# A gated delta-rule block on one Trainium2 core: the weights' preparation moved from a setup stage into the hand-written scheduler

## The chip, the cores and the metric

The kernel runs on one core of one Trainium2 chip. The metric is device microseconds of one execution; three timed executions of the kernel before gave 3868.83, 3886.9 and 3894.53 us, and their median, 3886.9 us, is the time before. A separate execution was recorded by the hardware profiler; the trace and every duration below come from it.

## The reference

Two residual sub-blocks, each with a LayerNorm in front and behind, over x of 8 batches, 1024 tokens, 128 features, all in float32. The first is a gated delta-rule attention with 16 heads (key size 64, value size 128); the second is a small feed-forward mix.

```python
q = l2(silu(causal_conv4(x @ Wq.T, conv_q)));  k = l2(silu(causal_conv4(x @ Wk.T, conv_k)))
v = silu(causal_conv4(x @ Wv.T, conv_v))
alpha = exp(-exp(A_log) * softplus(x @ Wa.T + dt_bias));  beta = 2 * sigmoid(x @ Wb.T)
# per token and head:
S = a_t * (S - b_t * k_t (k_t . S)) + k_t v_t;   o_t = S . q_t
attn = rms_norm(o) @ Wo.T
x = x + layernorm(attn(layernorm(x)))
# feed-forward on y = layernorm(x), y_prev = y shifted by one token:
out = sigmoid((mu_r*y + (1-mu_r)*y_prev) @ W_r.T) * (relu((mu_k*y + (1-mu_k)*y_prev) @ W_k.T)**2 @ W_v.T)
x = x + layernorm(out)
```

## The kernel before

**Tiling.** The recurrence is computed in chunks of 128 tokens. A unit is one batch, one half of its tokens (512) and one group of four heads: 8 x 2 x 4 = 64 units, in that order.

**Setup.** Constants come first: identities, triangular masks, `neg_a`, `dtb`, `mu` (lines 366 to 415). Then, in lines 425 to 480, a pool called `setup` loads all the weights and transposes them on TensorE, since the matmuls need them with the 128 features on the partitions. The three feed-forward matrices go to `wf` and the two gate matrices to `wab`. Wq, Wk (512 KB each), Wv and Wo (1 MB each) come in pieces of 512 KB through a staging tile `wt` (or `wot`) with two buffers, so the third piece's load waits until the first has been transposed. Each PSUM bank of up to four transposes is copied out by ScalarE and VectorE in turn (lines 358 and 360). For each group of four value heads the last is treated otherwise: its four convolution taps are multiplied into the weights by GpSimd (line 462, 16 products in all), transposed, and kept as four matrices in `wv`, so that its convolution is done by TensorE as four accumulated matmuls. The three loads of the taps (line 443) are issued on ScalarE's DMA queue, everything else on SyncE's.

**After the setup** the pool `mem` is opened on the space that `setup` gave up. GpSimd zeroes `tt` (two buffers), `tn` and `xs16` (line 500), and two DMAs write zeros from `xs16` to a DRAM scratch `td` (line 503).

**The scheduler.** All other work is 16 Python generators ("streams"), interleaved by a planner, class `Flow`, when the kernel is built. Each `yield part(engine, reads, resources, when)` says what the next piece needs: an engine, data written, free buffers of a kind, and a condition. `Flow` keeps a modelled clock per engine. In each turn it works out the earliest start of every stream's next piece, and among those within 0.3 us (`NEAR`) of the earliest it takes the stream that is least advanced by its own "due" count: each stream starts with a given due number and gains 1/parts with each piece. It adds 1.0 us (`SLACK`) between a write and a read on another engine, and it models the TensorE clock in windows of 3.4133 us. The order that results is fixed on every engine's queue; instructions of the streams are emitted through helpers, so the profile gives them all line 234. `begins` (due 1.2) runs once for a batch: it loads x by halves of 512 tokens into `xs` (one buffer), takes mean and variance on VectorE, a power on GpSimd, normalizes, transposes on TensorE into `xnT`, then computes the gates (`wabT` matmuls, softplus, cumulative sums, exponentials, two transposes) and sends `rowd` to DRAM. Only when a batch's `begins` is through may its convolutions (`keys` and `values`, both through `conv`) be placed: `conv` multiplies `xnT` by one transposed weight tile `wT[:, m]` and applies the taps on VectorE. `directs` uses `wv`, and `projects` uses `woT` and, at a half's end, `wfT`.

Staging tiles that the change uses are the scheduler's own: `mt` (two buffers, 128 x 16 x 128, used by `products` to `levels`) and `o` (two buffers, 128 x 4 x 128, used by `norms` and `projects`).

Of the kernel before, what the change touches and what calls it, by code (L numbers as in the profile page):

```python
# [8 lines left out]
F32 = mybir.dt.float32  # L9
AF = mybir.ActivationFunctionType  # L10
ALU = mybir.AluOpType
# [4 lines left out]
P = 128  # L16
H, DK, DV, KW = 16, 64, 128, 4
G = 4
NG = H // G
# [4 lines left out]
NVT = 1  # L24
# [3 lines left out]
NQ = H * DK  # L28
# [6 lines left out]
class Flow:  # L35
# [110 lines left out]
    def give(self, kind, tile_):  # L146
        if tile_.space == PSUM:
            kind, tile_ = self.of.pop(tile_.tensor.name, (kind, tile_))
        self.free.setdefault(kind, []).append(tile_)
# [70 lines left out]
def part(eng, *reads, when=None, spare=0, **takes):  # L220
    return eng, reads, takes, when, spare
# [76 lines left out]
def kernel(  # L298
# [51 lines left out]
    def quads(t):  # L350
        return t.rearrange("p (a b) -> p a b", b=P)

    turn = [0]

    def evac(dst, src):
        turn[0] += 1
        if turn[0] % 2:
            nc.scalar.copy(dst, src)
        else:
            nc.vector.tensor_copy(dst, src)  # L360

    spare = [0]

    def bank(name):
        spare[0] += 1
        return psums[spare[0] % len(psums)][:, 0:512]


    ident = const.tile([P, G, P], F32, tag="ident", name="ident")
    for i in range(G):  # L370
# [51 lines left out]
    woT = const.tile([P, H, D], F32, tag="woT", name="woT")  # L422
    wabT = const.tile([P, 2 * H], F32, tag="wabT", name="wabT")
    wfT = const.tile([P, 3, D], F32, tag="wfT", name="wfT")
    with tc.tile_pool(name="setup", bufs=2) as sp:
        wf = sp.tile([P, 3, D], F32, tag="wf", name="wf", bufs=1)
        for i, w in enumerate((W_r, W_k, W_v)):
            nc.sync.dma_start(wf[:, i, :], w)
        wab = sp.tile([2 * H, D], F32, tag="wab", name="wab", bufs=1)
        nc.sync.dma_start(wab[0:H, :], Wa)  # L430
        nc.sync.dma_start(wab[H : 2 * H, :], Wb)
        pw = bank("pw_ab")
        nc.tensor.transpose(pw[:, : 2 * H], wab, ident1[: 2 * H, : 2 * H])
        nc.vector.tensor_copy(wabT, pw[:, : 2 * H])
        pw = bank("pw_f")
        for i in range(3):
            nc.tensor.transpose(quads(pw)[:, i, :], wf[:, i, :], ident1)
        nc.vector.tensor_copy(wfT, quads(pw)[:, 0:3, :])

        n = 0  # L440
        for name, w, cw in (("q", Wq, conv_q), ("k", Wk, conv_k), ("v", Wv, conv_v)):
            nt = w.shape[0] // P
            nc.scalar.dma_start(taps[:, n : n + nt, :], cw.rearrange("(n p) k -> p n k", p=P))
            for g in range(nt // 8):
                wt = sp.tile([P, 8, D], F32, tag="wt", name=f"wt_{name}{g}")
                nc.sync.dma_start(
                    wt, w[g * 1024 : (g + 1) * 1024, :].rearrange("(n p) d -> p n d", p=P)
                )
                for i in range(2):
                    pw = bank(f"pw_{name}{g}_{i}")  # L450
                    for j in range(4):
                        if name != "v" or j < G - NVT:
                            nc.tensor.transpose(quads(pw)[:, j, :], wt[:, 4 * i + j, :], ident1)
                    if name != "v":
                        evac(wT[:, n : n + 4, :], quads(pw))
                    elif NVT < G:
                        m = 2 * NQ // P + (2 * g + i) * (G - NVT)
                        evac(wT[:, m : m + G - NVT, :], quads(pw)[:, : G - NVT])
                    for j in range(G - NVT if name == "v" else G, G):
                        scaled = sp.tile([P, KW, D], F32, tag="scaled", name=f"ws_{g}{i}{j}")  # L460
                        for k in range(KW):
                            nc.gpsimd.tensor_tensor(
                                scaled[:, k, :], wt[:, 4 * i + j, :],
                                taps[:, n + j, k : k + 1].broadcast_to([P, D]), ALU.mult,
                            )
                        pw = bank(f"pw_t{g}_{i}_{j}")
                        for k in range(KW):
                            nc.tensor.transpose(quads(pw)[:, k, :], scaled[:, k, :], ident1)
                        evac(wv[:, 2 * g + i, :, j - (G - NVT), :], quads(pw))
                    n += 4  # L470
        for g in range(2):
            wot = sp.tile([P, 8, DV], F32, tag="wt", name=f"wot_{g}")
            nc.sync.dma_start(
                wot, Wo[:, g * 8 * DV : (g + 1) * 8 * DV].rearrange("d (h v) -> d h v", v=DV)
            )
            for i in range(2):
                pw = bank(f"pw_o{g}_{i}")
                for j in range(4):
                    nc.tensor.transpose(quads(pw)[:, j, :], wot[:, 4 * i + j, :], ident1)
                evac(woT[:, g * 8 + 4 * i : g * 8 + 4 * i + 4, :], quads(pw))  # L480

    mem = ctx.enter_context(tc.tile_pool(name="mem", bufs=1))
# [64 lines left out]
    stock("rs", 2, [P, NC])  # L549
    stock("st", 2, [P, 6])  # L550

    units = [(b, hf, g) for b in range(B) for hf in range(NH) for g in range(NG)]
    gs = {}
    st = [dict(at=[]) for _ in units]
# [21 lines left out]
    def begins():  # L576
        for b in range(B):
# [25 lines left out]
                give("bank", pt)  # L603
                give("xs", xs)

            yield part("PE", xnT, bank=1)
            pab = take("bank")
            ab = pab[:, : NC * 2 * H].rearrange("p (c k h) -> p c k h", k=2, h=H)
            for c in range(NC):
# [63 lines left out]
    def conv(n, u, done, m=None):  # L673

        b, hf, _ = u
        m = n if m is None else m
        yield part("PE", bank=1, spare=2, when=lambda: len(done) < 2)
        pp = take("bank")
        xT = gs[b]["xnT"][:, KW - 1 + hf * TU : KW - 1 + (hf + 1) * TU]
        pe.matmul(pp, wT[:, m, :], xT, start=True, stop=True)  # L680
        yield part("ACT", pp, acc=1, pb=1)
        acc, pb = take("acc"), take("pb")
        ac.copy(pb[:, KW - 1 :], pp)
        ac.activation(acc, pp, AF.Copy, scale=taps[:, n, KW - 1 : KW])
        give("bank", pp)

        yield part("POOL", *([pb] if hf < NH - 1 else []))
        if hf:
            po.tensor_copy(pb[:, : KW - 1], edge[:, m, :])
        else:  # L690
            po.memset(pb[:, : KW - 1], 0.0)
        if hf < NH - 1:
            po.tensor_copy(edge[:, m, :], pb[:, TU:])
        for j in range(KW - 1):
            yield part("DVE", acc, pb)
            ve.scalar_tensor_tensor(
                acc, pb[:, j : j + TU], taps[:, n, j : j + 1], acc, ALU.mult, ALU.add
            )
        give("pb", pb)
        done.append(acc)  # L700
# [4 lines left out]
    def keys():  # L705
        for n, u in enumerate(units):
            b, hf, g = u
            yield part("PE", when=lambda: b in gs)
            for pr in range(NP):
                yield from conv(NQ // P + g * NP + pr, u, kq_done)  # L710
                yield from conv(g * NP + pr, u, kq_done)
# [97 lines left out]
    def directs():  # L809
        for n, u in enumerate(units):  # L810
            b, hf, g = u
            a = st[n]
            for c in range(CU if NVT else 0):
                t0 = hf * TU + c * P
                yield part("PE", bank=1, when=lambda: "vr" in a)
                xnT = gs[b]["xnT"]
                pv = take("bank")
                for j in range(KW):
                    pe.matmul(
                        pv[:, : NVT * DV], xnT[:, t0 + j : t0 + j + P],  # L820
                        wv[:, g, j].rearrange("p h v -> p (h v)"), start=j == 0, stop=j == KW - 1,
                    )
                yield part("ACT", pv)
                v = a["vr"][:, c, G - NVT :, :]
                ac.activation(v, pv[:, : NVT * DV].rearrange("p (h v) -> p h v", v=DV), AF.Silu)
                give("bank", pv)
                yield part("POOL", v)
                po.tensor_tensor(
                    v, v, a["r"][:, c, G - NVT :, None].broadcast_to([P, NVT, DV]), ALU.mult
                )  # L830
            prog["directs"] += 1
# [404 lines left out]
    def projects():  # L1236
        for u in units:
            b, hf, g = u
            for c in range(CU):
                yield part("PE", when=lambda: normed_outs)  # L1240
                o = normed_outs.pop(0)
                yield part("PE", o, bank=1)
                pt = take("bank")
# [118 lines left out]

    with tc.manual_schedule():
        flow.run([
            (begins(), 4.75, 1.2), (keys(), 25, 0.9), (lengths(), 16, 1.0), (products(), 16, 2.0),
            (rows(), 16, 2.9), (directs(), 12, 2.9), (values(), 19, 2.9), (blocks(), 17, 3.0),
            (decays(), 8, 3.2), (gathers(), 3, 3.2), (scatters(), 3, 3.2), (levels(), 18, 3.5),
            (prepares(), 16, 3.9), (steps(), 26.5, 4.0), (norms(), 32, 4.2), (projects(), 28.75, 4.2),
        ])
# [29 lines left out]
```

## Time and profile before

| what | value |
|---|---|
| timed executions (median) | 3868.83, 3886.9, 3894.53 us (3886.9) |
| profiled execution, own time | 3905.89 us |
| its span in the trace | 3903.8 us |
| DVE, ACT, POOL busy | 69%, 60%, 62% of the span |
| granted TensorE clock, mean | 0.945 of full |
| DMA traffic | 186.28 MB, mean 48 GB/s |

The profiled execution took 2.1 us more than its span, and 19.0 us more than the median. Engines: PE is the matmul part of TensorE and PEld its weight load, DVE is VectorE, ACT ScalarE, POOL GpSimd, SP SyncE. An engine name with a q (SPq, ACTq) is its queue issuing a DMA. A row of the timeline gives start, duration, engine, line, operation, output and inputs, count, and in brackets how long the engine had been idle before and what released it. The table by stretches gives, for each stretch of time, its length, the busy time and instruction count of each engine, the granted clock, the mean busy share of the 16 DMA engines and GB/s.

### The profile page before, as it was taken

Reading aid. Unit: us, or ns where it says so; the run is one execution under the profiler, and the core shown is the slowest. Engines: PE = TensorE matmul, PEld = TensorE weight load, DVE = VectorE, ACT = ScalarE, POOL = GpSimd, SP = SyncE. Lnnn points to the kernel's source line nnn. Section 1 sums busy time; section 2 is a strip of 40 time slices with the busy share of each in tenths; the row PEclk is TensorE's granted clock in tenths of the full one; section 3 lists DMA queues with packets and bytes.
Section 4 is the critical chain, followed back from the end, with each engine's and each line's share of the span. In section 5 each row is a group of like instructions: output and inputs, shape, how many; then the busy total and the mean of one; then the engine's idle time right before and its main releaser. Section 6 shows DMA issues by size and latency. Waiting matters only on the chain. (4 is left out here: it accounts for less than half of the span.)

```text
span 3903.8 us, 126873 instructions
## 1 busy us (share of the span) xinstructions
PE 3497.1 (90%) x52848; PEld 2672.6 (68%) x52848; DVE 2712.1 (69%) x5021; ACT 2323.4 (60%) x5774; POOL 2432.3 (62%) x4369
## 2 busy tenths in 40 slices
PE   5799998999989999999998899888998999989886
PEld 3576776767767776776776677666776667766675
DVE  5667667687776777777776677766677677667752
ACT  4466665656657566666656666565565666556452
POOL 3656666576666666667666576656666566666652
PEclk8899998999999999999999999899999999989997
DMA  3222222222222222222222222221222222222210
GB/s 77 54 43 42 56 47 47 52 45 49 51 50 46 54 46 44 58 52 42 50 54 44 45 51 48 48 48 38 56 44 51 48 42 51 51 41 49 46 36 11
DMA packets 712863, 186.28 MB, mean 48 GB/s; under 512 B 573120, under 2 KB 679008, under 8 KB 712288
## 3 DMA queue, kind: packets, MB, share of 16 engines
q1 hardware_dynamic: 708144, 178.11, 22.1%
q8 instruction: 415, 6.80, 0.7%
q14 instruction: 160, 1.31, 0.1%
q10 hardware_dynamic: 4144, 0.07, 0.1%
HBM read 138.18 MB, written 23.07 MB: 41 GB/s over the span
## 5 line engine op out<-in xcount | busy, mean ns | idle before, releaser
L234 DVE SCALAR_TENSOR_TENSOR acc<-pb,taps,acc 128x512 f32<-128x512 f32 x1344 | 1102.9, 823 | 211.5 <-ACT acc L234 105.1
L234 PE MATMUL bank<-xnT,wT 128*128 128x512 f32 x886 | 496.9, 649 | 12.2 <-ACT acc L234 5.3
L234 POOL TENSOR_TENSOR qk<-qk,egb 128x256 f32<-128x256 f32 x256 | 213.9, 836 | 450.4 <-PE pair L234 428.0
L234 POOL TENSOR_TENSOR vr<-vr,r 128x128 f32<-128x128 f32 (+1 forms) x448 | 355.4, 797 | 208.7 <-ACT vr L234 207.1
L234 POOL TENSOR_TENSOR nb<-nb,tmp 128x14 f32<-128x14 f32 (+6 forms) x896 | 334.7, 374 | 70.2
L234 ACT COPY pb<-bank 128x512 f32<-128x512 f32 x443 | 257.6, 581 | 202.6 <-PE bank L234 156.2
L234 POOL TENSOR_TENSOR tmp<-nb 128x14 f32<-128x14 f32 (+6 forms) x896 | 327.4, 365 | 48.1
L234 ACT COPY o<-pair 128x512 f32<-128x512 f32 x256 | 150.1, 586 | 340.4 <-PE pair L234 250.5
L234 DVE TENSOR_TENSOR_SCAN at<-at,ident 128x512 f32<-128x512 f32 x256 | 337.0, 1317 | 20.8 <-DMA at<-rowd 20.0
L234 PEld LDWEIGHTS bank<-tn,mt 64*64 64x64 f32 (+1 forms) x14192 | 282.9, 112 | 91.9 <-issue 25.0
L234 ACT ACTIVATE junk<-o 128x128 f32<-128x128 f32 x1024 | 317.3, 310 | 28.3
L234 PE MATMUL pair<-vr,tt 128*128 128x128 f32 x2048 | 297.6, 291 | 40.0 <-ACT tt L234 35.1
L234 PE MATMUL bank<-tn,mt 64*64 64x64 f32 (+1 forms) x14192 | 315.9, 191 | 19.4 <-DVE tn L234 4.7
L234 POOL TENSOR_TENSOR o<-o,so 128x512 f32<-128x512 f32 x256 | 320.8, 1253 | 19.1
L234 PE MATMUL bank<-woT,oT 128*128 128x128 f32 x2040 | 293.6, 288 | 20.8 <-ACT oT L234 16.9
L234 PEld LDWEIGHTS pair<-vr,tt 128*128 128x128 f32 x2048 | 264.5, 202 | 68.7 <-ACT tt L234 38.4
L234 PEld LDWEIGHTS bank<-woT,oT 128*128 128x128 f32 x2040 | 259.5, 197 | 72.8 <-ACT oT L234 24.6
L234 ACT ACTIVATE acc<-bank,taps 128x512 f32<-128x512 f32 x443 | 307.1, 693 | 0.3
L234 PE MATMUL pair<-w,at 128*128 128x128 f32 x2048 | 296.6, 290 | 2.3 <-issue 1.9
L234 PE MATMUL pair<-qk 64*128 64x256 f32 x2048 | 293.3, 405 | 4.8 <-ACT o L234 2.6
L234 POOL TENSOR_TENSOR so<-so,mhalf 128x4 f32<-128x4 f32 x256 | 280.4, 1095 | 20.1
L234 PEld LDWEIGHTS pair<-w,at 128*128 128x128 f32 x2048 | 262.5, 199 | 31.8 <-issue 20.8
(235 smaller groups left out, 7524.7 us busy)
## 6 DMA issues: line engine op xcount, KB each, us to landing
at<-rowd SPq DMA_DIRECT2D x256, 256.0 KB, 3.3
egb<-rowd SPq DMA_DIRECT2D x512, 64.0 KB, 3.2
tq<-td SPq DMA_DIRECT2D x256, 64.0 KB, 2.6
tt<-tq SPq DMA_DIRECT2D x256, 64.0 KB, 2.4
md<-mt SPq DMA_DIRECT2D x512, 16.0 KB, 1.8
nb<-md SPq DMA_DIRECT2D x64, 128.0 KB, 2.1
td<-nb SPq DMA_DIRECT2D x128, 64.0 KB, 3.1
xs<-in_L_attn_x_dram SPq DMA_DIRECT2D x16, 256.0 KB
```

The source lines that it names most:

```text
L234: res = call(*args, **kw)
```

## The change

The setup pool goes, with its helpers `evac` and `bank`. A 17th stream, `weights`, does the same loads, transposes and copies through the planner, with due number 0.0 and 1000 parts, so its count stays below that of every other stream. The taps' loads move from ScalarE's queue to SyncE's. Wk and Wq are loaded into one `mt` tile and all of Wv into the other, with no wait between them; Wo goes into the second when Wv has been transposed. The small matrices share one `o` tile, and the scaled value weights use the other. Key and query weights are transposed two at a time, in turn. A set `loaded` gates the streams that need weights, piece by piece.

```diff
-    with tc.tile_pool(name="setup", bufs=2) as sp:
-        wf = sp.tile([P, 3, D], F32, tag="wf", name="wf", bufs=1)
...
-                evac(woT[:, g * 8 + 4 * i : g * 8 + 4 * i + 4, :], quads(pw))
+    loaded = set()
+
+    def weights():
+        n = 0
+        yield part("SP")
+        for cw in (conv_q, conv_k, conv_v):
+            nt = cw.shape[0] // P
+            sy.dma_start(taps[:, n : n + nt, :], cw.rearrange("(n p) k -> p n k", p=P))
+            n += nt
+        yield part("SP", o=1)
+        small = take("o")
+        sy.dma_start(small[0:H, 3], Wa)
+        sy.dma_start(small[H : 2 * H, 3], Wb)
+        for i, w in enumerate((W_r, W_k, W_v)):
+            sy.dma_start(small[:, i], w)
+        yield part("PE", small[: 2 * H, 3], bank=1)
+        pw = take("bank")
+        pe.transpose(pw[:, : 2 * H], small[: 2 * H, 3], ident1[: 2 * H, : 2 * H])
+        yield part("DVE", pw)
+        ve.tensor_copy(wabT, pw[:, : 2 * H])
+        give("bank", pw)
+        loaded.add("ab")
+
+        yield part("SP", mt=2)
+        first, second_ = take("mt"), take("mt")
+        wide = lambda w: w.rearrange("(n p) d -> p n d", p=P)
+        nq = NQ // P
+        sy.dma_start(first[:, :nq], wide(Wk))
+        sy.dma_start(first[:, nq:], wide(Wq))
+        for i in range(2):
+            half_ = slice(i * nq, (i + 1) * nq)
+            sy.dma_start(second_[:, half_], wide(Wv[i * NQ : (i + 1) * NQ, :]))
+        last = G - NVT
+        for i in range(4):
+            for k in range(2):
+                m = (1 - k) * nq + 2 * i
+                yield part("PE", first[:, k * nq + 2 * i], bank=1)
+                pw = take("bank")
+                for j in range(2):
+                    pe.transpose(quads(pw)[:, j, :], first[:, k * nq + 2 * i + j], ident1)
+                yield part(("ACT", "DVE")[k], pw)
+                copy = (ac.copy, ve.tensor_copy)[k]
+                copy(wT[:, m : m + 2, :], quads(pw)[:, 0:2])
+                give("bank", pw)
+                loaded.update((m, m + 1))
+        give("mt", first)
+        for g in range(NG):
+            yield part("PE", second_[:, g * G], bank=1)
...
+            loaded.update(range(m, m + last))
+            for j in range(last, G):
+                yield part("POOL", second_[:, g * G + j], o=1)
+                scaled = take("o")
+                for k in range(KW):
+                    po.tensor_tensor(
+                        scaled[:, k, :], second_[:, g * G + j],
+                        taps[:, 2 * nq + g * G + j, k : k + 1].broadcast_to([P, D]), ALU.mult,
+                    )
...
+            loaded.add(("v", g))
+        yield part("SP")
+        for g in range(NG):
+            sy.dma_start(
+                second_[:, g * G : (g + 1) * G],
+                Wo[:, g * G * DV : (g + 1) * G * DV].rearrange("d (h v) -> d h v", v=DV),
+            )
...
+            loaded.add(("o", g))
+        give("mt", second_)
...
-            yield part("PE", xnT, bank=1)
+            yield part("PE", xnT, bank=1, when=lambda: "ab" in loaded)
...
-        yield part("PE", bank=1, spare=2, when=lambda: len(done) < 2)
+        yield part("PE", bank=1, spare=2, when=lambda: len(done) < 2 and m in loaded)
...
-                yield part("PE", bank=1, when=lambda: "vr" in a)
+                yield part("PE", bank=1, when=lambda: "vr" in a and ("v", g) in loaded)
...
-                yield part("PE", when=lambda: normed_outs)
+                yield part("PE", when=lambda: normed_outs and ("o", g) in loaded)
...
-            (begins(), 4.75, 1.2), (keys(), 25, 0.9), (lengths(), 16, 1.0), (products(), 16, 2.0),
+            (weights(), 1000, 0.0), (begins(), 4.75, 1.2), (keys(), 25, 0.9), (lengths(), 16, 1.0), (products(), 16, 2.0),
```

More of the change, by code (lines that the diff above doesn't have):

```diff
@@ L351, in quads @@
         return t.rearrange("p (a b) -> p a b", b=P)
[L353 to L366, printed above, removed]
     ident = const.tile([P, G, P], F32, tag="ident", name="ident")
@@ L424 @@
     wfT = const.tile([P, 3, D], F32, tag="wfT", name="wfT")
-    with tc.tile_pool(name="setup", bufs=2) as sp:
-        wf = sp.tile([P, 3, D], F32, tag="wf", name="wf", bufs=1)
[L427 to L479, printed above, removed]
-                evac(woT[:, g * 8 + 4 * i : g * 8 + 4 * i + 4, :], quads(pw))
@@ L550 @@
     stock("st", 2, [P, 6])
+    loaded = set()
[44 more added lines that the diff above has]
+            yield part("PE", second_[:, g * G], bank=1)
+            pw = take("bank")
+            for j in range(last):
+                pe.transpose(quads(pw)[:, j, :], second_[:, g * G + j], ident1)
+            yield part("ACT", pw)
+            m = 2 * nq + g * last
+            ac.copy(wT[:, m : m + last, :], quads(pw)[:, :last])
+            give("bank", pw)
+            loaded.update(range(m, m + last))
[7 more added lines that the diff above has]
+                    )
+                yield part("PE", scaled, bank=1)
+                pw = take("bank")
+                for k in range(KW):
+                    pe.transpose(quads(pw)[:, k, :], scaled[:, k, :], ident1)
+                give("o", scaled)
+                yield part("DVE", pw)
+                ve.tensor_copy(wv[:, g, :, j - last, :], quads(pw))
+                give("bank", pw)
+            loaded.add(("v", g))
[5 more added lines that the diff above has]
+            )
+        yield part("PE", small, bank=1)
+        pw = take("bank")
+        for i in range(3):
+            pe.transpose(quads(pw)[:, i, :], small[:, i], ident1)
+        give("o", small)
+        yield part("DVE", pw)
+        ve.tensor_copy(wfT, quads(pw)[:, 0:3, :])
+        give("bank", pw)
+        for g in range(NG):
+            yield part("PE", second_[:, g * G], bank=1)
+            pw = take("bank")
+            for j in range(G):
+                pe.transpose(quads(pw)[:, j, :], second_[:, g * G + j], ident1)
+            yield part("ACT", pw)
+            ac.copy(woT[:, g * G : (g + 1) * G, :], quads(pw))
+            give("bank", pw)
+            loaded.add(("o", g))
+        give("mt", second_)
```

## The prediction

> **What bounds the kernel now.** I read the page first, then the table by stretches for the batches, then the first 53 us in the timeline. The page's line of engines:
>
> ```profile
> PE 3497.1 (90%) x52848; PEld 2672.6 (68%) x52848; DVE 2712.1 (69%) x5021; ACT 2323.4 (60%) x5774; POOL 2432.3 (62%) x4369
> ```
>
> TensorE is the bound over the whole. The stretches below are cut where each batch's last output goes out (650.04, 1107.01, 1575.83, 2046.39, 2521.99, 2989.30, 3474.07 and 3900.36 us in the timeline of SyncE's queue):
>
> ```profile
> 650.00:1107.00 457.00, 422.75 (x6365) 324.55 (x6364) 332.33 (x615) 292.94 (x733) 304.58 (x543) 0.98 0.24 49
> 1107.00:1576.00 469.00, 426.61 (x6785) 325.54 (x6785) 341.94 (x629) 284.90 (x706) 301.70 (x537) 0.96 0.24 49
> 2046.00:2522.00 476.00, 435.32 (x6601) 332.78 (x6603) 337.45 (x627) 289.37 (x721) 305.54 (x544) 0.95 0.23 48
> 2989.00:3474.00 485.00, 440.63 (x6638) 338.57 (x6626) 345.97 (x636) 291.55 (x726) 306.33 (x546) 0.95 0.23 48
> ```
>
> In the steady state PE is busy for 91 to 93% of each batch. But batches of equal work take 457 to 485 us: the planner's order differs from batch to batch. All this comes after the part that the change touches, which is the start:
>
> ```profile
> 0.00:27.00 27.00, 12.95 (x64) 10.01 (x64) 5.96 (x12) 5.55 (x10) 8.82 (x37) 0.94 0.52 128
> 27.00:53.00 26.00, 8.18 (x36) 6.58 (x35) 7.60 (x30) 5.89 (x13) 7.56 (x10) 0.52 0.13 41
> ```
>
> Two stretches stand one after the other: 27 us of weights with DMA half busy, then 26 us of the first batch's norms and gates, in which no engine is busy for a third of the time and the DMA hardly at all. The timeline says why they do not overlap:
>
> ```profile
> 12.82 2.03 SPq L446 DMA_DIRECT2D wt_v<-in_L_attn_Wv_dram  x2
> 16.78 5.77 POOL L462 TENSOR_TENSOR ws<-wt_v,taps 128x128 f32<-128x128 f32 x16 [13.04 <-DMA wt_v<-in_L_attn_Wv_dram]
> 27.05 0.38 SPq L234 DMA_DIRECT2D xs<-in_L_attn_x_dram  x1
> 27.14 3.56 POOL L500 MEMSET tt<- 128x2048 f32 x2 [4.58 <-PE pair L479]
> 32.07 0.81 SPq L503 DMA_DIRECT2D td<-xs  x2
> 34.83 0.38 SPq L234 DMA_DIRECT2D xs<-in_L_attn_x_dram  x1
> 53.00 8.12 PE L234 MATMUL bank<-xnT,wT 128*128 128x512 f32 x12
> ```
>
> The first x load and the memsets wait for the setup's last transposes, which end at 27.0 us, and whose space they take over. The chain of `begins` is x0 issued at 27.05, x1 at 34.83 (7.8 us later, `xs` having one buffer), first convolution at 53.00 (18.2 us later).
>
> **The change part by part.**
>
> *Removed: the wait for the setup's space.* x0 is then held only by what is ahead of it on SyncE's queue. The constants' four issues end at 2.61. The taps' three issues come over from ScalarE's queue: 0.45 + 0.60 + 1.52 = 2.6 us, to 5.2. Five small matrices took from 2.65 to 5.99, 3.3 us, to 8.5. The planner's 0.5 us an issue puts x0 here, ahead of Wk. So x0 goes out at about 8.5, unless the two zero writes `td` stand in front. They wait for memsets: those take 3.56 + 0.96 + 0.53 = 5.05 us on POOL and can start when its constants end, at 3.7, so they end at 8.8; with 0.8 us for the two writes and 5.9 us of taps and small loads behind, x0 would go out at 15.5. In the trace x0 (27.05) passed `td` (32.07) while its memset was unfinished, so I take 8.5 and keep 15.5.
>
> *Moved: 2 MB of loads beside `begins`.* In the setup, Wq was issued at 6.24 and landed 4.5 us later, and Wk was there by 12.5, so a second 512 KB adds some 1.8 us. Behind x0 (half that size, 0.9 us), Wk and Wq go out at 8.9 and 9.4 and land near 14.3 and 16.1; Wv follows by 20. x0 itself is ahead of them.
>
> *Added waits in the fixed orders.* The planner, with 1.0 us of slack per hop, puts the 16 transposes of Wk and Wq ahead of x0's four transposes on PE. On the chip they wait for Wq: from 16.1, at 0.25 to 0.27 us each (8 in 1.97, 4 in 1.07), they end near 20.3. x0's would have started 6.7 us after the issue (33.71 - 27.05), at 15.2. Queued behind are x0's normalizing (two `xn` buffers) and with it x1's load. This costs `begins` 5 us. On POOL the 16 products (5.77 us) are planned after the first power, and between them it is idle: at worst one group (4 x 0.36 = 1.4 us) stands before the second power. The Wv and Wo transposes, 44 x 0.27 = 12 us, go into 18 us in which PE is mostly idle; copies of 0.5 to 0.7 us on ACT and DVE likewise. For these I take 2.5 us, between 0 and 5.
>
> *Sum.* First convolution: 8.5 + 7.8 + 5 + 18.2 + 2.5 = 42.0 us instead of 53.0: **11 us less**. With no interference: 8.5 + 26 = 34.5, 18.5 us less. With `td` in front and all interference, 15.5 + 7.8 + 5 + 18.2 + 5 = 51.5, 1.5 us less; if in addition the first power were behind the products that need Wv, some 4 us more, a loss of 2.5. From the first convolution on all work follows it, so what is gained there is kept if the order stays as good. Against the profiled execution: 3905.9 - 11 = 3894.9, a factor of 0.9972; on the median, **3876 us**.
>
> *The taps' queue.* ScalarE's queue shows 4144 packets for 0.07 MB, the last third landing 4.3 us after its issue; on SyncE's queue they are ahead of the gate weights and x0. The Trainium skill, page "DMA: Bandwidth & Descriptors", section "Issuing engines are not separate DMA queues", says that issuing from several engines saves only sequencer time, as all transfers run on the same 16 engines. By that the move costs the 2.6 us counted above. That row's 4.3 us allows more: taps issued until 5.2 are done at 9.5, a us after x0's issue, which I leave inside the 2.5 us.
>
> *The TensorE clock.* The granted clock fell from 0.94 in the setup to 0.52 in `begins`, and the first convolutions ran at 0.86 us instead of 0.43. I count nothing for this, as PE has room beside `begins`. The Trainium skill, page "TensorE: Matmul & The Clock Gate", section "HAM oscillation — how this bites in real kernels", says that idle gaps of over about 3.4 us halve the clock; that speaks against scattering transposes, and by it the 44 late ones would take some 0.42 us each (0.42 is the mean of the Wq transposes in the groups by line), 6.6 us more, and the sum would be a gain of 4 us.
>
> *The order of the other 16 streams.* None of their pieces changes, but the planner now reaches the first convolution with other engine clocks and another phase of its windows, and every later choice can fall otherwise. The rows bound this: the six full batches take 457, 469, 470, 476, 467 and 485 us, mean 470.7, standard deviation 9.3. If seven batches were new draws, their sum would move by 9.3 x 2.65 = 25 us, and the difference of two such sums by 35. Matmul counts of 6245 to 6857 in these stretches show that part of the spread is only where the cut falls, so 35 is too much; I take 25. Its mean is nothing.
>
> **The rivals.**
>
> *A better order besides.* A batch of 457 and PE's idle time of 33 to 45 us in a batch show that there is room. 4 us less in each of seven batches, with the 11, makes 39 us, the 1%: some 3840 us. Against it: nothing in the change aims there.
>
> *A worse order.* The place is the steady state, the mechanism the same reshuffled queue order. Batches at 478 instead of 470.7 cost 7 x 7.3 = 51 us, less 11: 3927 us. It decides from 7.1 us a batch on; the slowest row, 485, is twice as far out. Against it: the chance of so many bad batches at once, and PE's 91% leaves only so much to lose.
>
> *No overlap in fact.* If the fixed orders make `begins` wait for the weights piece after piece, the first convolution stays near 51 to 55 us: 3885 to 3890 us.
>
> **How the numbers follow.** Likeliest: 11 us gained, order about as good, 3876 us, 0.53 (3850 to 3905 by itself). Better order 0.24, worse order 0.15, no overlap 0.08. A 1% of 3887 is 39 us, about what a measurement of this kernel can tell from no change. So faster by over 1%: 0.24; within: 0.53 + 0.08 = 0.61; slower: 0.15. The range takes the likeliest case and the nearer half of both orders' cases: 3822 to 3926 us.
>
> **What would show it.** Right: x0's load at 8 to 9 us, x1's at 19 to 24, the first convolution at 38 to 46; transposes of Wk and Wq on PE ahead of x0's, released by a DMA; batches again between 457 and 485. Wrong in the start: `td` before the taps on SyncE's queue, x0 after 15, POOL's power behind the products, or the first convolution after 50. Wrong in the rest: the distance from the first convolution to the end (3850.8 us before) changes by more than 28 us; then the order, not the start, makes the result.

## The result and the profile after

The changed kernel takes 3851.9 us (median of 6 runs, 3844.9 to 3861.1) against 3890.2 us before (6 runs, 3868.8 to 3897.3): a ratio of 0.9907 [0.9887, 0.9928], 0.9% or some 36 to 38 us faster. The forecast was 11 us. The range held the time, and the 1% that the prediction put between "faster" and "no change" was just not reached; the interval crosses it.

The profiled execution took 3852.50 us, its span is 3850.8. Its line of engines on the page:

```profile
PE 3465.8 (90%) x52848; PEld 2662.8 (69%) x52848; DVE 2709.6 (70%) x5021; ACT 2325.4 (60%) x5779; POOL 2433.2 (63%) x4369
```

The same 52848 matmuls kept PE busy 31 us less, and it was idle for 385.0 us instead of 406.7 (span minus busy). The start, from the timeline:

```profile
7.54 0.43 SPq L234 DMA_DIRECT2D xs<-in_L_attn_x_dram  x1
8.11 0.53 POOL L428 MEMSET xs<- 128x512 f32 x1
12.54 2.24 SPq L431 DMA_DIRECT2D td<-xs  x2
12.57 0.69 PE L234 MATMUL bank<-ident,mt 128*128 128x128 f32 x2 [4.58 <-DMA mt<-in_L_attn_Wk_dram]
14.50 2.82 PE L234 MATMUL bank<-ident,mt 128*128 128x128 f32 x12 [1.24 <-DMA mt<-in_L_attn_Wq_dram]
17.12 0.40 PE L234 MATMUL bank<-ident,xn 128*128 128x128 f32 x1
18.89 0.38 SPq L234 DMA_DIRECT2D xs<-in_L_attn_x_dram  x1
34.67 2.03 ACT L234 COPY woT<-bank 128x512 f32<-128x512 f32 x4
36.70 1.28 ACT L234 ACT_TABLE_LOAD   x1
38.00 0.28 ACT L234 ACTIVATE eg<-bank 128x128 f32<-128x128 f32 x1
39.55 7.87 PE L234 MATMUL bank<-xnT,wT 128*128 128x512 f32 x12
```

x0 now goes out at 7.54 us, x1 at 18.89, and the first convolution starts at 39.55 instead of 53.00: 13.45 us earlier. The transposes of Wk and Wq stand ahead of x0's on PE, held by their loads, as forecast. But the rest of the run also became shorter. From the first convolution to the end it took 3850.8 us before and 3811.25 now, 39.6 us less in these two executions. The one of before was 16 us above its median; by the medians, 38 us less in all and 13 at the start, some 25 us are left for the rest. The table by stretches says where they lie; the two stretches are the start, and the last batch from the seventh's last output to its own. Before:

```profile
0.00:53.00 53.00, 21.13 (x99) 16.59 (x99) 13.56 (x42) 11.44 (x22) 16.39 (x47) 0.73 0.33 85
3474.07:3900.36 426.29, 358.77 (x5509) 282.86 (x5507) 235.83 (x457) 220.86 (x579) 226.11 (x398) 0.90 0.18 36
```

and after:

```profile
0.00:39.55 39.55, 19.27 (x99) 16.18 (x99) 12.99 (x42) 12.43 (x26) 16.42 (x47) 0.85 0.45 114
3441.68:3847.51 405.83, 347.19 (x5382) 273.60 (x5381) 234.57 (x455) 221.45 (x580) 227.14 (x398) 0.94 0.19 38
```

The last batch is 20.5 us shorter. PE's idle time there fell from 67.5 to 58.6 us and its busy time by 11.6, with a granted clock of 0.94 instead of 0.90. With 127 fewer matmuls left after the seventh batch's output, some 8 us of the 20.5 (an estimate, 127 at the row's mean of 0.065 us) are work that now lies ahead of the cut. The last batch comes 3400 us after the weights; the planner's order is what reaches so far. That was the theory to test.

### The profile page after: what moved, and what is told of

Its sections match the earlier page's. It is cut to its first block, busy times and chain, and to the rows that moved or that the text cites. A ratio compares the mean times of both kernels' runs of the same rounds, so it can differ in the third digit from the quotient of the medians.

```text
span 3850.8 us, 126886 instructions
## 1 busy us (share of the span) xinstructions
PE 3465.8 (90%) x52848; PEld 2662.8 (69%) x52848; DVE 2709.6 (70%) x5021; ACT 2325.4 (60%) x5779; POOL 2433.2 (63%) x4369
## 5 line engine op out<-in xcount | busy, mean ns | idle before, releaser
L234 DVE SCALAR_TENSOR_TENSOR acc<-pb,taps,acc 128x512 f32<-128x512 f32 x1344 | 1088.7, 812 | 208.5 <-ACT acc L234 108.6
L234 PE MATMUL bank<-xnT,wT 128*128 128x512 f32 x878 | 488.4, 645 | 4.1 <-ACT tt L234 2.7
L234 PEld LDWEIGHTS bank<-tn,mt 32*32 32x32 f32 (+1 forms) x14176 | 281.3, 111 | 96.8 <-issue 26.4
L234 PE MATMUL bank<-tn,mt 32*32 32x16 f32 (+1 forms) x14176 | 314.1, 191 | 20.1 <-ACT acc L234 5.6
L234 PE MATMUL bank<-woT,oT 128*128 128x128 f32 x2032 | 286.6, 285 | 20.5 <-ACT oT L234 17.6
L234 DVE TENSOR_TENSOR mt<-pair,at 128x512 f32<-128x512 f32 x256 | 175.9, 687 | 164.3 <-PE pair L234 105.8
```

The lines of the kernel that those rows point to most:

```text
L234: res = call(*args, **kw)
```

## The experiments

**Crossing start and order.** The streams' order was written down, as the sequence of choices that the planner made in each kernel, and then replayed in place of its own choice. In both kernels the first 38 pieces of `begins` (and, in the changed one, all 52 of `weights`) come before any other stream, so the sequences can be cut there and crossed. Beyond the cut every engine's queue holds the same instructions in the same order as the kernel that it was taken from. The edit in both kernels:

```diff
     def run(self, streams):
...
-            near = min(could)[0] + self.NEAR
-            k = min(x[1:] for x in could if x[0] <= near)[1]
-            s = waiting[k][0]
...
+        for c in ORDER:
+            s, (eng, reads, takes, when, spare) = waiting[c]
...
             need = next(s, None)
```

> The changed kernel with its start (weights beside the first norms and gates), but from the first convolution on every engine's queue in the order of the kernel before. Theory ORDER (13.5 us come from the earlier first convolution, the other 25 from the order in which the other streams now fall): first convolution near 39.6 us, 3890 - 13.5 = 3877 us, ratio 0.9965. Rival START (the overlap itself is worth all 38 us, for example by a warmer clock or a better filled pipeline): 3852 us, ratio 0.991.

Measured: 3875.7 us, ratio 0.9964 [0.9946, 0.9983]; the first convolution at 40.02 us.

> The kernel before with its setup in front, but from the first convolution on every queue in the order of the changed kernel. ORDER: first convolution at 53 us, 3890 - 25 = 3865 us, ratio 0.9936, the last batch shorter than before as in the changed kernel (406 us against 426 between the last two batches' final outputs). START: 3890 us, ratio 1.000.

Measured: 3869.0 us, ratio 0.9944 [0.9923, 0.9965]; the first convolution at 52.94 us. START falls with both. The product of the two ratios is 0.9908, the changed kernel's is 0.9907: start and order add up. The start's part is 0.36% (14 us, by its interval 7 to 21), the order's 0.56% (22 us, 14 to 30); that the order's is the larger is likely, but the intervals overlap. The same two stretches show it, first for the new start with the old order, then for the old start with the new order:

```profile
0.00:40.02 40.02, 19.21 (x98) 16.12 (x99) 12.94 (x42) 12.42 (x26) 16.43 (x47) 0.85 0.45 113
3456.31:3879.51 423.20, 360.06 (x5511) 283.99 (x5509) 235.46 (x457) 220.65 (x579) 224.46 (x397) 0.90 0.18 37
```

```profile
0.00:52.94 52.94, 20.79 (x99) 16.17 (x100) 13.48 (x42) 11.43 (x22) 16.34 (x47) 0.73 0.33 85
3469.28:3872.44 403.16, 347.39 (x5385) 273.27 (x5383) 234.94 (x455) 221.45 (x580) 225.86 (x398) 0.93 0.19 38
```

The first stretch goes with the start (40 or 53 us), the last batch with the order (423 to 426 us or 403 to 406). Between the first convolution and the seventh batch's end the four kernels take 3421, 3416, 3402 and 3416 us (before, new start with old order, after, old start with new order). That stretch does not sort them by order: the two with the same new order differ by 14. Over the whole, PE was busy for 3497.1, 3496.5, 3465.8 and 3477.1 us in the same sequence: 31 of the 32 us that the new order takes off behind the new start, and 20 of the 28 behind the old one, are time in which the same 52848 matmuls ran shorter, not time in which PE waited less. The mean granted clock of the four executions (0.945, 0.946, 0.951, 0.945) goes with this behind the new start alone, so why they ran shorter is not settled.

**Is the better order a merit of the change?** Six kernels, before or after, in which only the planner's modelled clocks begin at another time (0.3, 3.0 and 6.0; 2.1, 2.4 and 8.0), so that its phase and near ties fall otherwise and no work changes:

```diff
-        self.now = dict(PE=0.0, DVE=0.0, ACT=0.0, POOL=0.0, SP=0.0)
+        self.now = dict(PE=0.3, DVE=0.3, ACT=0.3, POOL=0.3, SP=0.3)
```

> The changed kernel, only the planner's modelled clocks begin at 0.3 instead of 0, which redraws the order and leaves the start's work. The planner's own model makes this order 35 us longer than that of the changed kernel (a model's number, not a time). ORDER: the overlap's 13 us remain, the rest is a new draw: 3870 to 3890 us, 3885 if the chip follows the model. START: 3852 us again, within 5.

Measured: 3850.6 us, ratio 0.9898 [0.9876, 0.9920]. It equals the changed kernel, as START said, and ORDER's 3870 to 3890 us was missed, though the crossed kernels speak against START; the planner's model, which made this order longer, was no guide.

> The kernel before, only the planner's modelled clocks begin at 2.4 instead of 0. The planner's model makes this order 19 us shorter (a model's number, not a time). ORDER: some 3871 us, ratio 0.995, with nothing changed in the start. START: 3890 us, ratio 1.000 within 0.002.

Measured: 3875.9 us, ratio 0.9965 [0.9946, 0.9985]: a better order without the change. With two orders of the changed kernel at 3851 us, it stayed open whether the weights' stream as such leads to better orders; four more draws put that question.

> The changed kernel with the planner's modelled clocks beginning at 3.0; the start's work is the same. Theory DRAW (the order gained or lost by a change of phase is a matter of chance, with a spread of some 10 us): anywhere from 3850 to 3885 us, the 13 us of the start kept, so below 3890. Rival SYSTEMATIC (with the weights as a stream the planner always finds an order better by some 25 us): 3851 us within 5, as with the clocks at 0 and 0.3.

Measured: 3882.6 us, ratio 0.9987 [0.9970, 1.0005], although its first convolution starts at 39.69 us.

> As the one with 3.0, the clocks beginning at 6.0. DRAW: 3850 to 3885 us. SYSTEMATIC: 3851 us within 5.

Measured: 3864.5 us, ratio 0.9952 [0.9937, 0.9967].

> The kernel before with the planner's modelled clocks beginning at 2.1. DRAW: 3864 to 3900 us, another value than 3889 and 3876. SYSTEMATIC: 3876 to 3890 us, the orders without the weights' stream staying behind by 25 us once the start's 13.5 us are taken off.

Measured: 3885.1 us, ratio 1.0007 [0.9985, 1.0029].

> The kernel before with the planner's modelled clocks beginning at 8.0. DRAW: 3864 to 3900 us; one of the two draws under 3870 would show that the order of the changed kernel is in reach without the change. SYSTEMATIC: 3876 to 3890 us.

Measured: 3910.9 us, ratio 1.0059 [1.0038, 1.0079], although the planner's model made this order 24 us shorter. That is above DRAW's 3900 us as well, and no draw of the kernel before came under 3870.

SYSTEMATIC falls with the start at 3.0: the same change with another phase gains next to nothing. But these kernels are fewer draws than they look. Before at 2.1, after at 3.0 and after at 6.0 have one and the same order: behind the start, their traces show the same operations on the same tiles in the same sequence on DVE, ACT, POOL and SyncE's queue, and the last batch has the same counts, which differ in every other order. The rows of the last batch for these three, named in that sequence:

```profile
3472.70:3876.14 403.44, 354.23 (x5435) 279.21 (x5435) 241.51 (x465) 222.70 (x584) 238.53 (x401) 0.94 0.19 39
3465.98:3876.07 410.09, 359.81 (x5435) 282.87 (x5435) 241.00 (x465) 222.79 (x584) 238.05 (x401) 0.93 0.19 38
3459.54:3864.84 405.30, 355.26 (x5435) 278.75 (x5435) 240.88 (x465) 222.76 (x584) 237.76 (x401) 0.93 0.19 39
```

So with and without the stream of weights the planner can find this order, here called C, and behind the old start it is no better than the first (1.0007). In one table, with a letter for each order (the crossed kernels have A behind the new start and B behind the old one), with the time from the first convolution to the end of batch 7 and the last batch from each profiled execution:

| kernel, planner's clocks begin at | order | ratio to before | first convolution, us | to the end of batch 7, us | last batch, us |
|---|---|---|---|---|---|
| before, 0 | A | 1 | 53.00 | 3421 | 426 |
| before, 2.1 | C | 1.0007 | 52.86 | 3420 | 403 |
| before, 2.4 | D | 0.9965 | 52.68 | 3413 | 404 |
| before, 8.0 | E | 1.0059 | 52.62 | 3432 | 427 |
| after, 0 | B | 0.9907 | 39.55 | 3402 | 406 |
| after, 0.3 | F | 0.9898 | 39.86 | 3401 | 401 |
| after, 3.0 | C | 0.9987 | 39.69 | 3426 | 410 |
| after, 6.0 | C | 0.9952 | 36.43 | 3423 | 405 |

The change fixes the first convolution (at 6.0 the start's own pieces fell 3 us better as well), and not the two columns that follow it. The profiled execution of the first row is 16 us above its kernel's median, the others are within 6 of theirs. The ratios of the kernel before spread over 0.94%, those of the changed kernel over 0.89%. Their means, 1.0008 and 0.9936, differ by 0.72% where the start alone is worth 0.35% (13.45 of 3890 us). With four orders on one side, three on the other and C on both, the 0.37% that are left neither show nor exclude that the stream of weights leads to slightly better orders on average.

Order C is also a second crossing of the start. Against before at 2.1, a first convolution 13.2 us earlier gave 0.20% (8 us), and one 16.4 us earlier 0.55% (21 us). Between the two changed kernels lie 3.3 us of the first convolution but 18 us of the median, on one chip and with intervals that do not meet. Some 15 us are thus explained neither by the start nor by the order; the mean granted clock of the timed executions was 0.949 and 0.952, and why they differ stays open. A single pair of kernels should not be trusted below that; the start's 14 and the order's 22 us come out alike on two sides each of the first crossing.

**What else the start can give.** Two kernels replay a start written by hand: x0's load first of all, its norms ahead of the transposes of Wk and Wq on PE, the second power ahead of the value products on POOL, and Wo's transposes among the first convolutions. The third kernel of the group is the changed one again.

```diff
-ORDER = "wwbbwwwbwwwwwwwbbwwwwbwwbbwwwwbbwwwbbwwbwwbbwwww"
+ORDER = "bbwwwwwbbbbbbbbbbbbbwwwwwwwwwwwwwwwwbbbbbbbbbbbb"
...
```

A letter is one piece, w of `weights` and b of `begins`; these are the first 48, above as the planner chose them in the changed kernel, below as written by hand.

> The changed kernel with another order of the start alone: x0's load ahead of the taps and the small matrices, x0's norms ahead of the transposes of Wk and Wq on PE, the second power ahead of the value products on POOL, the Wo transposes among the first convolutions; from the first convolution on the order of the changed kernel. If the 5 us and 2.5 us of waits that the prediction put on the first norms and the seven issues ahead of x0 are real, x0 goes out at 2.7 us, x1 near 12.5, the first convolution starts near 32 instead of 39.6, and the time is 7 us less than the changed kernel's: 3845 us, ratio 0.989. Rival (the first convolution is held by something else, such as the landing of the weights or the clock): 38 us or later, 3852 us.

Measured: 3851.4 us, ratio 0.9897 [0.9865, 0.9929]. The first convolution was at 36.11 us, 3.4 earlier instead of 7.6:

```profile
2.67 0.43 SPq L383 DMA_DIRECT2D xs<-in_L_attn_x_dram  x1
8.89 0.28 PE L383 MATMUL bank<-ident,o 32*128 32x32 f32 x1 [8.89 <-DMA o<-in_L_attn_Wb_dram]
9.21 0.19 DVE L383 COPY wabT<-bank 128x32 f32<-128x32 f32 x1 [3.95 <-PE bank L383]
14.88 0.40 SPq L383 DMA_DIRECT2D xs<-in_L_attn_x_dram  x1
20.06 0.29 DVE L383 BATCH_NORM_STATS2 st<-xs 128x6 f32<-128x128 f32 x1 [2.10 <-DMA xs<-in_L_attn_x_dram]
```

x0 did go out at 2.67 us, but x0's statistics were queued on DVE behind the gate weights' copy at 9.21, and x1 went out behind Wv and `td` and was used 5.2 us later, against 2.9 in the kernel before. A wait taken out on one queue was replaced by another. The time cannot tell 3.4 us: the unaltered changed kernel on the same chip had 0.9915, and the intervals overlap.

> The same start before the order that the planner finds when its clocks begin at 0.3 (3851 us with the changed kernel's start). The gain of the start and the luck of the order add up, so 3844 us, ratio 0.988; if they do not, 3851.

Measured: 3841.6 us, ratio 0.9872 [0.9848, 0.9896], the first convolution at 36.08 us; against 0.9898 with the ordinary start, 3.8 us earlier at the first convolution. The sign is right, the intervals overlap.

> The changed kernel, unaltered, on the same chip as the two with the other start: 3852 us, ratio 0.991 within 0.002.

Measured: 3857.0 us, ratio 0.9915 [0.9893, 0.9937]; the last batch 406 us again.

The last kernel loads the second half of the first batch's x into the residual buffer, which is idle then, so that both halves go out ahead of all weights:

```diff
-                yield part("SP", xs=1)
-                xs = take("xs")
+                kind = "xr" if c0 and not b else "xs"
+                yield part("SP", **{kind: 1})
+                xs = take(kind)
...
-                give("xs", xs)
+                give(kind, xs)
```

> The changed kernel, with the order that the planner finds when its clocks begin at 0.3, and another start: both halves of the first batch's x are loaded ahead of all weights, the second half into the idle residual buffer; all norms and the gate matmuls stand ahead of the weights' transposes; the last two value groups and Wo go among the first convolutions. If a microsecond by which the first convolution starts earlier is a microsecond of the total, as in the crossed kernels: first convolution near 28 us instead of 39.9, 12 us less than the 3851 us of that order, 3839 us, ratio 0.987. Rival (a start this early only moves the wait into the first batch's pipeline, whose later stages need the weights): first convolution near 28 us but 3845 to 3851 us.

Measured: 3829.8 us, ratio 0.9847 [0.9815, 0.9879], the fastest of all, 63.6 us less than before on the same chip. From its timeline:

```profile
3.13 0.52 SPq L383 DMA_DIRECT2D xr<-in_L_attn_x_dram  x1
8.77 1.03 POOL L383 TENSOR_TENSOR rs<-rs,mhalf 128x4 f32<-128x4 f32 x1
14.25 1.02 POOL L383 TENSOR_TENSOR rs<-rs,mhalf 128x4 f32<-128x4 f32 x1 [4.45 <-DVE rs L383]
23.92 0.29 DVE L383 TENSOR_TENSOR la<-e,neg_a 128x128 f32<-128x128 f32 x1
25.64 0.63 PE L383 MATMUL bank<-la,upper 128*128 128x128 f32 x2
30.09 1.88 PE L383 MATMUL bank<-xnT,wT 128*128 128x512 f32 x4
```

The first convolution starts at 30.09 us, 9.8 earlier than with the same later order and the ordinary start; the first power starts as soon as its input (8.68 us) and the memsets ahead of it on POOL (8.72 us) are done, and the cumulative sums, whose input is ready at 24.21, start at 25.64 behind the transposes of Wk and Wq. The ratio fell by 0.0051 against that order's 0.9898, about 20 us, with half-widths of 12 and 9 us: that it is more than 0 is plain, and the rival's 3845 us lie outside the interval; that it is more than the 9.8 is not shown.

## Why the prediction was right, and where it was off

**The start: right, though two terms lay elsewhere.** The forecast first convolution was 42.0 us, measured 39.55; the gain 11 us against 13.45. x0 went out at 7.54 instead of 8.5: the taps' three issues took 1.7 us on SyncE's queue (2.6 on ScalarE's), and `td` did stay behind, at 12.54. Wq was there at 14.50 instead of 16.1. Its transposes held x0's, which began at 17.12, 9.6 us after the issue instead of 6.7: a wait of 2.9 us, not 5. Part of this wait was on DVE, where x0's normalizing, its power done at 13.62, stood behind copies of the weights until 16.42.

From x1's issue to the first convolution it took 20.66 us, against the 18.2 + 2.5 = 20.7 of the sum. The 2.5 was right in size, and two pieces make it. Seven transposes of the scaled value weights stand ahead of the gates' matmuls on PE, which start 1.5 us later behind x1's issue than before. And a table load is no longer hidden: before, it ran beside DVE and PE work; now Wo's copies (34.67 to 36.70) stand in front of it on ScalarE, and `eg` starts 1.5 us after the cumulative sums end (36.52) instead of at once. The cumulative sums themselves took 0.7 us less. Before:

```profile
42.71 3.46 PE L234 MATMUL bank<-wabT,xnT 128*128 128x32 f32 x16
49.08 1.28 ACT L234 ACT_TABLE_LOAD   x1
51.45 0.28 ACT L234 ACTIVATE eg<-bank 128x128 f32<-128x128 f32 x1 [1.09 <-PE bank L234]
```

and after, with Wo's transposes in the last row:

```profile
26.81 1.70 PE L234 MATMUL bank<-ident,o 128*128 128x128 f32 x7
28.30 3.46 PE L234 MATMUL bank<-wabT,xnT 128*128 128x32 f32 x16
31.57 3.33 PE L234 MATMUL bank<-ident,mt 128*128 128x128 f32 x16
```

**That a microsecond of the start is one of the total: right on average.** With the order held fixed, 13.0 us at the first convolution gave 14 us (7 to 21) in the first crossing; order C gave 8 us for 13.2 and 21 for 16.4.

**The order: the term was mis-sized.** The prediction set its mean to nothing and its spread to 25 us, and so named 11 us as the likeliest gain. Measured with the start held fixed, it gave 22 us, twice the 11. So what happened is nearer the rival "a better order besides" (0.24) than the likeliest case (0.53), though the time still lies in the likeliest case's own range of 3850 to 3905 us. That the 1% was not passed is luck as much as insight: the start's 14 and the order's 22 us make nearly that rival's 39. (That rival's time is 3887 - 39 = 3848 us, not the 3840 that the prediction wrote.) The prediction's own sign for this case, a change of more than 28 us behind the first convolution, showed in the two traces (39.6 us), and by the medians just did not (25). The spread as such was about right: the six orders, with 0.35% added back for the new start and the three values of C averaged, lie between 0.993 and 1.006, a standard deviation of 18 us, or 26 for the difference of two.

**The place: wrong, and in part open.** The prediction drew the spread from the differences between full batches and priced both rivals per batch, 4 or 7 us in each of seven. In the crossed kernels the new order saves 17 us (new start) and 23 us (old start) in the last batch, where the stages run dry. No row of the full batches shows that stretch, although the table by stretches had it (426 us with a clock of 0.90). But a short last batch does not make a fast kernel: order C has one of 403 to 410 us and gains nothing by it, since its earlier batches take longer than those of B and F. Which choices of the planner make an order fast is not settled.

**The two pages of the skill.** On the taps' move, the Trainium skill, page "DMA: Bandwidth & Descriptors", section "Issuing engines are not separate DMA queues", says that issuing from several engines only saves sequencer time. The trace agrees: the move cost 1.7 us of issue, and 0.7 more on the issue behind them (1.17 us for Wa instead of 0.43), while x0 was used 3.07 us after its issue against 2.95 before. On the clock, its page "TensorE: Matmul & The Clock Gate", section "HAM oscillation — how this bites in real kernels", warns of idle gaps on TensorE, and the prediction took from it a price of 0.42 us for each transpose that is scattered. The row of Wo's shows no such harm: 16 in 3.33 us, 0.21 each. The stretch before the first convolution had a mean clock of 0.85, against 0.73 before. At the first convolutions it was 0.50 in both kernels, and their first six matmuls start 0.86 us apart in both.

## What to carry to other kernels

When a greedy planner fixes the order of everything, an edit at its start re-rolls the order of all that follows. Here that was worth plus or minus 0.5%, more than the edit itself: replay the old order behind the new start, and the new order behind the old start, before crediting the edit. Several draws of the planner's phase cost one changed constant each and show how much of a gain is luck; check that they are different orders. And price the run-out of the pipeline on its own: full batches say nothing about it.

## What was not expected of the hardware

The executions of one kernel differ by up to 1%, and the difference goes with the granted TensorE clock. For the kernel with both halves of x first, 3825.6 us at 0.957 and 3850.8 us at 0.952; for the one with x0 first, 3828.6 at 0.954, 3849.6 at 0.950 and 3866.4 at 0.943. In these two, 0.001 of mean clock goes with some 3 to 5 us, with program and data the same. What sets the clock of one execution is not shown.
